# Layer norms moved from GpSimd to VectorE, with a new order of two woven streams

## The chip, the core and the metric

The kernel runs on one core of a Trainium2 chip. A core has five engines with instruction queues of their own: TensorE (PE in the profile; PEld is its weight load), VectorE (DVE), the scalar engine (ACT), GpSimd (POOL) and SyncE (SP), which here issues the DMAs. The metric is device microseconds of one execution. Matmuls write to PSUM, and the scores, products and transposes of this kernel share four PSUM slots of 128x1024 float32.

## The reference

`x` is (8, 512, 256) and the context `ctx` is (8, 1024, 192). Four residual blocks follow each other; the normed `x` of each has no learned scale:

```python
def _layernorm(x, axis=-1, eps=1e-05):
    m = jnp.mean(x, axis=axis, keepdims=True)
    v = jnp.var(x, axis=axis, keepdims=True)
    return (x - m) / jnp.sqrt(v + eps)
...
x = x + L0_xattn(_layernorm(x), ctx)   # cross attention, 16 heads of 64
x = x + L0_ffn(_layernorm(x))          # 2 of 8 experts, chosen from token 0 of each batch element
x = x + L1_xattn(_layernorm(x), ctx)   # cross attention, 16 heads of 16; the keys are the values
x = x + L1_ffn(_layernorm(x))          # weights quantized to 8 bits, activations to 16 by one global maximum
```

The last block quantizes its normed input by the largest absolute value over all batches, so it can only start when every batch has been through the three blocks before it.

## The kernel before

**Tiles.** One batch's `x` is a tile `xs[b]` of 128 partitions by 4 x 256 (four token tiles). Three of them are alive. The main part works batch by batch, a batch taking some 395 us in the middle of the run.

**Two streams.** Two generators emit the program. Stream 1 is `first_attention` for all eight batches, then the last batch's experts and half of its second attention. Stream 2 first prepares the weights of the later blocks, then runs `rest(b)` for each batch: `experts(b)`, `second_attention(b)`, `last_norm(b)`. So the first attention of a later batch runs beside the later blocks of an earlier one. Each `yield` is a step, and the text `ORDER` at the head of the file says how many steps are taken from stream 1, then from stream 2, and so on; `weave` does just that:

```python
for n, count in enumerate(ORDER.split()):
    i = n % 2
    for _ in range(int(count)):
        ...
        heads[i] = next(streams[i], None)
```

The order of TensorE's instructions is the order in which steps emit them. The other engines' instructions are put in order by the framework's scheduler. The tuples that each `yield` hands out (engine, planned microseconds, kind of hold on a buffer) are a planner's costs, with which an order was planned; they emit nothing, nor does the constant `TURN`.

**Names that matter.** In the first attention, `scores` writes `s` (L728), VectorE reduces it to `least` (L739), the scalar engine takes the exponential `e` (L741), VectorE inverts its sum to `share` (L755), GpSimd divides with it (L758), TensorE turns `e` round into `t` (L676), and the scalar engine and VectorE each copy half into `et` (L690, L688) for the product `av` (L699). `queries` and `keys` write `pq` and `pk`, `values` writes `pv`. In the second attention `sm_c` (L524) are scores for the maxima `cmx` (L531), sent through DRAM and back as the stacked rows `ck` and `m_rows`; `cav` (L1079) is the product. `tc` (L457) transposes the context that `load_ctx` loads. `acc` (L486) is a block's last matmul; `add_to_x` then adds it to `x` on VectorE (L496). At the end of the main part `tmxx` (L1274) transposes the maxima of all batches for the global scale.

**The norm.** `layernorm_T` makes three steps: the norm itself, then two chunks that transpose the normed tile on TensorE (`txn`, L418) and copy it to `xT` (L422, L427). `norm_stats` takes mean and variance on VectorE (L384, L385), and the reciprocal root on GpSimd as three rounds of Newton's method from an integer guess (L387 to L398, 14 instructions on 128x4). `normed` then subtracts and multiplies, four instructions of 128x256 on GpSimd (L409). This happens three times per batch (24 times); `last_norm` needs only the root and the row ends (`ends`), because the last block norms again on VectorE from stored statistics (L1325). The normed tile lies in the pool of `e` tiles (16 buffers).

**Other work on GpSimd** is the division, the adding of biases to `x`, two small steps on `ends`, and some memsets.

Of the kernel before, what the change touches and what calls it, by code (L numbers as in the profile page):

```python
# [14 lines left out]
ALU = mybir.AluOpType  # L15
# [4 lines left out]
EPS = 1e-5  # L20
# [4 lines left out]


ORDER = """
15 4 11 1 1 4 3 2 2 1 5 4 3 1 8 1 6 1 3 1 3 1 3 1 1 1 1 1 6 1 3 1 1 1 1 1 1 1 3 1 1
1 1 1 3 1 1 1 5 1 1 1 3 1 1 1 1 1 3 1 1 1 1 1 1 1 3 1 1 1 1 1 1 1 4 1 91 1 4 4 6 1 3
2 6 2 4 2 7 5 4 2 1 1 4 1 1 1 1 5 1 1 5 2 3 7 1 3 6 2 3 7 1 1 1 2 6 2 3 10 1 4 1 1 5  # L30
2 3 7 1 1 1 2 5 2 1 1 1 1 3 2 2 3 5 2 1 1 3 1 1 2 4 9 2 1 3 2 11 2 4 1 7 2 2 1 3 6 3
1 1 1 5 1 1 2 4 2 5 4 6 1 4 1 2 1 3 1 1 1 5 2 3 4 6 1 3 2 6 2 4 2 7 5 4 2 1 1 4 1 1
1 1 5 1 1 5 2 3 7 1 3 6 2 3 7 1 1 1 2 6 2 3 10 1 4 1 1 5 2 3 7 1 1 1 2 5 2 1 1 1 1 3
2 2 3 5 2 1 1 3 1 1 2 4 9 2 1 3 2 11 2 4 1 7 2 2 1 3 6 3 1 1 1 5 1 1 2 4 2 5 4 6 1 4
1 2 1 3 1 1 1 5 2 3 4 6 1 3 2 6 2 4 2 7 5 4 2 1 1 4 1 1 1 1 5 1 1 5 2 3 7 1 3 6 2 3
7 1 1 1 2 6 2 3 10 1 4 1 1 5 2 3 7 1 1 1 2 5 2 1 1 1 1 3 2 2 3 5 2 1 1 3 1 1 2 4 9 2
1 3 2 11 2 4 1 7 2 2 1 3 6 3 1 1 1 5 1 1 2 4 2 5 4 6 1 4 1 2 1 3 1 1 1 5 2 3 4 6 1 3
2 6 2 4 2 7 5 4 2 1 1 4 1 1 1 1 5 1 1 5 2 3 7 1 3 6 2 3 7 1 1 1 2 6 2 3 10 1 4 1 1 5
2 3 7 1 1 1 2 5 2 1 1 1 1 3 2 2 3 5 2 1 1 3 1 1 2 4 9 2 1 3 2 11 2 4 1 7 2 2 1 3 6 3
1 1 1 5 1 1 2 4 2 5 4 6 1 4 1 2 1 3 1 1 1 5 2 3 4 6 1 3 2 6 2 4 2 7 5 4 2 1 1 4 1 1  # L40
1 1 5 1 1 5 2 3 7 1 3 6 2 3 7 1 1 1 2 6 2 3 10 1 4 1 1 5 2 3 7 1 1 1 2 5 2 1 1 1 1 3
2 2 3 5 2 1 1 3 1 1 2 4 9 2 1 3 2 11 2 4 1 7 2 2 1 3 6 3 1 1 1 5 1 1 2 4 2 5 4 6 1 4
1 2 1 3 1 1 1 5 2 3 4 6 1 3 2 6 2 4 2 7 5 4 2 1 1 4 1 1 1 1 5 1 1 5 2 3 7 1 3 6 2 3
7 1 1 1 2 6 2 3 10 1 4 1 1 5 2 3 7 1 1 1 2 5 2 1 1 1 1 3 2 2 3 5 2 1 1 3 1 1 2 4 9 2
1 3 2 11 2 4 1 7 2 2 1 3 6 3 1 1 1 5 1 1 2 4 2 5 4 6 1 4 1 2 1 3 1 1 1 5 2 3 4 6 1 3
2 6 2 4 2 7 5 4 2 1 1 4 1 1 1 6 1 1 2 4 1 1 1 3 1 2 1 3 2 1 1 2 3 3 2 5 1 1 2 6 2 3
2 1 1 6 4 5 1 1 2 6 2 3 2 1 1 7 1 4 4 5 2 4 1 7 1 5 2 3 1 2 2 3 7 1 3 4 2 3 7 2 2 1
1 1 1 1 11 2 1 1 1 1 5 1 8 1 2 3 3 1 2 1 7 3 2 4 3 8 3 1 5 2 1 7 2 3 7 2 3 7 2 3 7 3
3 9 3 2 9 3 2 6 2 1 2 1 2 1 3 1 4 2
"""  # L50


# [26 lines left out]
def kernel(  # L79
# [26 lines left out]
    nc = tc.nc  # L106
# [273 lines left out]
    def norm_stats(b, mv, rs):  # L380

        st = small.tile([P, NT, 6], F32, tag="st", name="st")
        for t in range(NT):
            nc.vector.bn_stats(st[:, t, :], xs[b][:, t, :])  # L384
            nc.vector.bn_aggr(mv[:, t, :], st[:, t, :])  # L385
        ve = small.tile([P, NT], F32, tag="ve", name="ve")
        nc.gpsimd.tensor_scalar(ve, mv[:, :, 1], EPS, None, ALU.add)  # L387

        r = small.tile([P, NT], F32, tag="r0", name="r0")
        nc.gpsimd.tensor_scalar(  # L390
            r.bitcast(I32), ve.bitcast(I32), -0.5, float(0x5F3759DF), ALU.mult, ALU.add
        )
        t1 = small.tile([P, NT], F32, tag="t1", name="t1")
        for i in range(3):
            nc.gpsimd.tensor_tensor(t1, r, r, ALU.mult)
            nc.gpsimd.tensor_tensor(t1, t1, ve, ALU.mult)
            nc.gpsimd.tensor_scalar(t1, t1, -0.5, 1.5, ALU.mult, ALU.add)
            nc.gpsimd.tensor_tensor(rs if i == 2 else r, r, t1, ALU.mult)  # L398

    def norm_of(b):  # L400
        mv = small.tile([P, NT, 2], F32, tag="mv", name="mv")
        rs = small.tile([P, NT], F32, tag="rs", name="rs")
        norm_stats(b, mv, rs)
        return mv, rs

    def normed(pool, tag, b, mean, rs):
        xn = pool.tile([P, NT, D], F32, tag=tag, name=f"xn_{b}")
        for t in range(NT):
            nc.gpsimd.tensor_scalar(  # L409
                xn[:, t, :], xs[b][:, t, :], mean(t), rs(t), ALU.subtract, ALU.mult  # L410
            )
        return xn

    def transposed_chunk(b, xn, xT, c, by_place=False):

        t = bank(f"txn_{b}_{c}")
        for i in range(NT):
            nc.tensor.transpose(  # L418
                t[:, i * P : (i + 1) * P], xn[:, i, c * P : (c + 1) * P], ident
            )  # L420
        if by_place:
            nc.scalar.copy(  # L422
                xT[:, c, :].rearrange("p (w r) -> p w r", w=CD),
                t.rearrange("p (r w) -> p w r", w=CD),
            )
        else:
            nc.scalar.copy(xT[:, c, :], t)  # L427
# [3 lines left out]
    def layernorm_T(b, xT, by_place=False):  # L431

        xn = []

        def norm():
            mv, rs = norm_of(b)
            xn.append(
                normed(pp, "e", b, lambda t: mv[:, t, 0:1], lambda t: rs[:, t : t + 1])
            )

        return [(1.3, [(0, None, "dve", 2.6, None), (0, None, "pool", 8.2, "then")], norm)] + [
            (
                ("done", 0) if c == 0 else 0,
                [(0.5, "s", "act", 0.6, "full")],
                lambda c=c: transposed_chunk(b, xn[0], xT, c, by_place),
            )
            for c in range(DH)
        ]
# [124 lines left out]
    def prologue(b):  # L573

        if b in loaded:
            raws = loaded.pop(b)
        else:
            load_x(b)
            raws = load_ctx(b)
        c1 = io.tile([P, L], F32, tag="c1", name=f"c1_{b}")  # L580
        c2 = io.tile([P, L // 2], F32, tag="c2", name=f"c2_{b}")
        contexts[b] = c1, c2
        xTs[b] = work.tile([P, DH, S], F32, tag="xT", name=f"xT_{b}", bufs=1)

        def bias():
            for i in range(NT):
                nc.gpsimd.tensor_tensor(xs[b][:, i, :], xs[b][:, i, :], bo_b, ALU.add)

        return layernorm_T(b, xTs[b]) + context_T(b, raws, c1, c2), bias

    def first_attention():
# [172 lines left out]
        VALUES = [(2.75, "s", "act", 1.03, "full")]  # L764
        OUT = [(3.44, "s", "dve", 1.25, "full")]
        BIAS = [(0, None, "pool", 2.9, "aside")]
        TURN = 0.55

        share = 1 / (NP * NT)

# [8 lines left out]
        def divided(g):  # L779
            return [  # L780
                (0, None, "dve", 0.2, None, (("y", g % 4),), None),
                (0, None, "pool", 4.8, "then", (), ("w", g % 4)),
            ]

        def turned_round(g, u):
            engine, took = ("dve", 1.22) if u else ("act", 1.03)
            return [(TURN, "s", engine, took, "rows", (("w", g % 4),), ("t", u, g % 4))]

# [10 lines left out]
        for n in range(last + 2):  # L799
# [5 lines left out]
            for i in range(NT):  # L805
                g = n * NT + i
# [130 lines left out]
    def second_attention(b, pairs, last=False):  # L937
# [172 lines left out]
        def turned(g, a):  # L1110

            t = bank(f"cta_{b}_{g}")
            flat = a.rearrange("p w d -> p (w d)")
            for c in range(DH):
                nc.tensor.transpose(t[:, tok(c)], flat[:, tok(c)], ident)
            aT = small.tile([P, D], F32, tag="aT", name=f"caT_{b}_{g}", bufs=1)
            nc.vector.tensor_copy(aT, t[:, :D])
            return aT
# [26 lines left out]
        JOIN = [(0.86, "s", "dve", 1.5, "columns")]  # L1145
        TURN = [(0.3, "s", "dve", 0.4, "full")]
        OUT = [(0.86, "s", "dve", 0.4, "full")]
# [20 lines left out]
        for p in pairs:  # L1168
            for kt in range(NK):
# [11 lines left out]
                if kt == 4:  # L1181
                    yield 0, HALF[0]
                    attend(p, 0)
                    if joining:
                        yield 0, TURN
                        a = turned(p // 2 - 1, a)
# [19 lines left out]
        a = joined(p1 // 2 - 1)  # L1206
        yield ("done", 0), TURN
        a = turned(p1 // 2 - 1, a)
# [4 lines left out]
    def last_norm(b):  # L1213


        yield 1, [(0, None, "dve", 5.5, None), (0, None, "pool", 4.5, "then")]
        mv = small.tile([P, NT, 2], F32, tag="mv", name="mv")
        norm_stats(b, mv, stats[:, b, :, 1])
        nc.vector.tensor_copy(stats[:, b, :, 0], mv[:, :, 0])
        for i, op_ in enumerate((ALU.max, ALU.min)):  # L1220
            nc.vector.tensor_reduce(ends[:, b, i, :], xs[b], AX.X, op_)
        for i in range(2):
            nc.gpsimd.tensor_tensor(
                ends[:, b, i, :], ends[:, b, i, :], stats[:, b, :, 0], ALU.subtract
            )
            nc.gpsimd.tensor_tensor(
                ends[:, b, i, :], ends[:, b, i, :], stats[:, b, :, 1], ALU.mult
            )
        yield ("done", 0), []
        xd[b] = dram.tile([P, NT, D], F32, name=f"xd{b}")  # L1230
        nc.sync.dma_start(out=xd[b], in_=xs[b])
        done.add((b, "stored"))
# [239 lines left out]
```

## Time and profile before

| What | Value |
|---|---|
| Median of 3 runs | 3412.78 us (3411.16 to 3414.15) |
| Profiled execution | 3413.37 us |
| Its span | 3411.5 us |
| Mean granted TensorE clock | 0.974 |
| Normed quarters on GpSimd (L409) | 96, 1222 ns each |
| Divisions on GpSimd (L758) | 512, 1894 ns each |

The span is the time from the first to the last instruction in the trace; the execution's own time contains 1.9 us more. In a group's line the form is engine, line, operation, tiles `out<-in`, shapes and count, then total busy microseconds and mean nanoseconds of one. In the timeline's lines start and length come first, and a bracket at the end gives the idle time before the instruction and what released it.

### The profile page before, as it was taken

To read this page: it belongs to the slowest core of one execution; us is meant where nothing else is said; L and a number is where in the kernel's file an instruction comes from. 1 tells how busy PE (TensorE), PEld (TensorE's weight loads), DVE (VectorE), ACT (ScalarE), POOL (GpSimd) and SP (SyncE) were. 2 spreads that over 40 slices of the span, in tenths; PEclk is the share of its full clock that TensorE was granted. 3 is DMA by queue.
4 is the path that set the end of the run, shared out by engine and by line. 5 is a ranking of instruction groups with operands and counts; after the bars stand their busy time and mean duration, and the time that the engine had idled before them with its cause. 6 is when DMAs were issued, how large, how long until landed. Compare 5 with 4: busy or idle time off the path is not lost.

```text
span 3411.5 us, 59285 instructions
## 1 busy us (share of the span) xinstructions
PE 3183.9 (93%) x24293; PEld 1789.0 (52%) x24293; DVE 2045.0 (60%) x2583; ACT 1857.9 (54%) x2589; POOL 1282.3 (38%) x1260
## 2 busy tenths in 40 slices
PE   7899999999999999999999999999999999978887
PEld 4455555555455555555545554555555555544347
DVE  3654566546665476655665466654766456656688
ACT  4554456544556455554655455554555546544578
POOL 4355522454234622355224542345223543311002
PEclk9999999999999999999999999999999999988989
DMA  2010111011110111111110111101111111012112
GB/s 86 26 32 21 45 33 37 27 41 41 38 35 27 43 32 36 35 44 29 32 51 14 41 41 38 41 26 38 32 41 32 41 32 29 14 44 62 50 57 81
DMA packets 102649, 132.00 MB, mean 39 GB/s; under 512 B 19807, under 2 KB 82028, under 8 KB 102252
## 3 DMA queue, kind: packets, MB, share of 16 engines
q1 hardware_dynamic: 102380, 128.22, 13.7%
q8 instruction: 192, 3.15, 0.4%
q14 instruction: 77, 0.63, 0.1%
HBM read 67.34 MB, written 9.96 MB: 23 GB/s over the span
## 4 chain that ended last, share of the span: by engine, by line
PE 74%; DVE 12%; ACT 6%; POOL 3%; issue 2%; DMA 1%; SPq 1%; ACTq 0%; DVEq 0%; POOLq 0%
PE s L728 15%; PE av L699 11%; PE cav L1079 6%; PE t L676 6%; DVE cmx L531 5%; PE acc L486 5%; PE pv L512 4%; PE s_c L562 3%; PE pq L602 3%; PE pk L512 3%; ACT e L741 2%; ACT e_c L567 2%; PE sm_c L524 2%; PE s_c L565 2%; PE pv L514 2%
## 5 line engine op out<-in xcount | busy, mean ns | idle before, releaser
L758 POOL TENSOR_TENSOR e<-e,share 128x1024 f32<-128x1024 f32 x512 | 958.9, 1894 | 1559.1 <-DVE share L755 1528.0
L741 ACT ACTIVATE e<-s,least 128x1024 f32<-128x1024 f32 x512 | 569.6, 1113 | 621.3 <-DVE least L739 590.0
L739 DVE TENSOR_REDUCE least<-s 128x1 f32<-128x1024 f32 x512 | 603.2, 1219 | 229.5 <-PE s L728 226.4
L531 DVE TENSOR_REDUCE cmx<-sm_c 128x2 f32<-128x1024 f32 x512 | 602.1, 1219 | 169.8 <-PE sm_c L524 169.2
L728 PE MATMUL s<-k,q 64*128 64x512 f32 x2048 | 586.6, 624 | 23.0 <-ACT et L690 8.8
L567 ACT ACTIVATE e_c<-s_c 128x1024 f32<-128x1024 f32 x512 | 499.7, 1024 | 112.9 <-PE s_c L565 101.8
L699 PE MATMUL av<-et,v 128*64 128x256 f32 x4096 | 472.2, 384 | 0.7 <-ACT et L690 0.7
L688 DVE COPY et<-t 128x1024 f32<-128x1024 f32 x256 | 312.8, 1222 | 230.4 <-PE t L676 228.5
L699 PEld LDWEIGHTS av<-et,v 128*64 128x64 f32 x4096 | 284.4, 137 | 219.4 <-issue 67.9
L728 PEld LDWEIGHTS s<-k,q 64*128 64x128 f32 x2048 | 237.1, 191 | 221.1 <-issue 118.1
L676 PEld LDWEIGHTS t<-ident,e 64*128 64x128 f32 x8192 | 294.4, 141 | 93.9 <-issue 68.2
L690 ACT COPY et<-t 128x1024 f32<-128x1024 f32 x256 | 260.1, 1016 | 151.4 <-PE t L676 149.9
L676 PE MATMUL t<-ident,e 64*128 64x64 f32 x8192 | 313.7, 227 | 18.1 <-ACT e_c L567 12.1
L562 PE MATMUL s_c<-cq,ck 64*128 64x512 f32 x1024 | 248.5, 476 | 16.1 <-ACT e_c L567 10.7
L524 PE MATMUL sm_c<-ck,cq 64*128 64x512 f32 x1024 | 228.5, 442 | 25.9 <-DMA ck<-ckl 12.5
L1079 PE MATMUL cav<-e_c,cv 128*32 128x512 f32 x2048 | 248.2, 599 | 2.2 <-DVE cmx L531 1.9
L755 DVE RECIPROCAL share<-total 128x2 f32<-128x2 f32 x256 | 42.5, 166 | 298.2 <-ACT e L741 297.8
L565 PE MATMUL s_c<-m_rows,m_ones 64*128 64x512 f32 x1024 | 208.6, 396 | 2.7 <-DMA m_rows<-mr_c 2.6
L562 PEld LDWEIGHTS s_c<-cq,ck 64*128 64x128 f32 x1024 | 99.3, 187 | 165.2 <-issue 39.4
L524 PEld LDWEIGHTS sm_c<-ck,cq 64*128 64x128 f32 x1024 | 98.8, 189 | 107.5 <-DVE cmx L531 38.4
L512 PE MATMUL pv<-wv,c 128*128 128x256 f32 x512 | 131.2, 399 | 3.7 <-DMA wv<-in_L_xattn_w_kv_dram 2.4
L512 PE MATMUL pk<-c,wk 128*128 128x512 f32 x256 | 126.8, 618 | 4.5 <-DVE et L688 2.7
(202 smaller groups left out, 3382.9 us busy)
## 6 DMA issues: line engine op xcount, KB each, us to landing
cq<-cqs SPq DMA_DIRECT2D x256, 64.0 KB
ck<-ckh SPq DMA_DIRECT2D x112, 128.0 KB
ck<-ckl SPq DMA_DIRECT2D x112, 128.0 KB
wq<-in_L_xattn_w_q_dram SPq DMA_DIRECT2D x32, 256.0 KB
wo<-in_L_xattn_w_out_dram SPq DMA_DIRECT2D x32, 256.0 KB
w<-in_L_ffn_W_dram SPq DMA_DIRECT2D x32, 256.0 KB
x<-xd SPq DMA_DIRECT2D x16, 512.0 KB
ctx<-in_ctx_dram SPq DMA_DIRECT2D x16, 384.0 KB
```

The lines of the kernel that those rows point to most:

```text
L512: nc.tensor.matmul(out, lhs, rhs, start=first, stop=False, skip_group_check=True)
L524: nc.tensor.matmul(s[:, h, :], q[half, tok(i)], k[half, g * 512 : (g + 1) * 512], start=True, stop=True,)
L531: nc.vector.tensor_reduce(mx[:, :, i, g], s, AX.X, ALU.max)
L562: nc.tensor.matmul(s[:, h, :], k[half, tok(kt)], q[half, :], start=True, stop=False)
L567: nc.scalar.activation(e, s, AF.Exp, scale=scale)
L676: nc.tensor.transpose(t[:, w, h, kt, :], es[n, i][h][half, tok(4 * u + kt)], ident[half, half],)
L699: nc.tensor.matmul(av[h * AD : (h + 1) * AD, : S // 2], v[m][:, 4 * u + kt, (at + h) * AD : (at + h + 1) * AD], turned[n, j, u][:, h, kt]. ...
L728: nc.tensor.matmul(s[h][:, g, :], q[n][half, tok(i)], k[n][half, g * 512 : (g + 1) * 512], start=True, stop=True,)
L739: nc.vector.tensor_reduce(least[:, h : h + 1], s[h], AX.XY, ALU.min)
L741: nc.scalar.activation(e, s[h].rearrange("p g n -> p (g n)"), AF.Exp, bias=least[:, h : h + 1], scale=-1.0, accum_out=total[:, h : h + 1],)
L758: nc.gpsimd.tensor_tensor(e, e, share[:, h : h + 1].to_broadcast([P, L]), ALU.mult)
L1079: nc.tensor.matmul(av[col : col + SL, :], va[:, v : v + SL], es[p, kt][:, h, :], start=(i == 0), stop=(i == NK // 4 - 1),)
```

## The change

It has three parts. The root of `norm_stats` runs on VectorE, with one small instruction fewer in each of its three rounds and one more ahead of them (12 in all). The four instructions of `normed` run on VectorE. `ORDER` is a new list, planned with new constants for the norm, the division, `TURN` and the last norm. GpSimd keeps the divisions, the biases, `ends` and the memsets. The line numbers of the changed file are 1 higher from the table on and 3 higher after `norm_stats`.

```diff
 ORDER = """
-15 4 11 1 1 4 3 2 2 1 5 4 3 1 8 1 6 1 3 1 3 1 3 1 1 1 1 1 6 1 3 1 1 1 1 1 1 1 3 1 1
...
+16 2 10 1 5 1 1 2 5 3 3 2 8 1 1 1 4 1 1 1 5 3 11 1 4 1 3 1 3 1 1 1 3 1 1 1 1 1 1 1 4
...
 """
...
         ve = small.tile([P, NT], F32, tag="ve", name="ve")
-        nc.gpsimd.tensor_scalar(ve, mv[:, :, 1], EPS, None, ALU.add)
+        nc.vector.tensor_scalar(ve, mv[:, :, 1], EPS, None, ALU.add)
 
         r = small.tile([P, NT], F32, tag="r0", name="r0")
-        nc.gpsimd.tensor_scalar(
+        nc.vector.tensor_scalar(
             r.bitcast(I32), ve.bitcast(I32), -0.5, float(0x5F3759DF), ALU.mult, ALU.add
         )
+        nc.vector.tensor_scalar(ve, ve, -0.5, None, ALU.mult)
         t1 = small.tile([P, NT], F32, tag="t1", name="t1")
         for i in range(3):
-            nc.gpsimd.tensor_tensor(t1, r, r, ALU.mult)
-            nc.gpsimd.tensor_tensor(t1, t1, ve, ALU.mult)
-            nc.gpsimd.tensor_scalar(t1, t1, -0.5, 1.5, ALU.mult, ALU.add)
-            nc.gpsimd.tensor_tensor(rs if i == 2 else r, r, t1, ALU.mult)
+            nc.vector.tensor_tensor(t1, r, r, ALU.mult)
+            nc.vector.tensor_tensor(t1, t1, ve, ALU.mult)
+            nc.vector.scalar_tensor_tensor(
+                rs if i == 2 else r, t1, 1.5, r, ALU.add, ALU.mult
+            )
...
         for t in range(NT):
-            nc.gpsimd.tensor_scalar(
+            nc.vector.tensor_scalar(
                 xn[:, t, :], xs[b][:, t, :], mean(t), rs(t), ALU.subtract, ALU.mult
             )
...
-        return [(1.3, [(0, None, "dve", 2.6, None), (0, None, "pool", 8.2, "then")], norm)] + [
+        return [(1.3, [(0, None, "dve", 6.0, None)], norm)] + [
...
-        TURN = 0.55
+        TURN = 0.52
...
-                (0, None, "pool", 4.8, "then", (), ("w", g % 4)),
+                (0, None, "pool", 4.0, "then", (), ("w", g % 4)),
...
-        yield 1, [(0, None, "dve", 5.5, None), (0, None, "pool", 4.5, "then")]
+        yield 1, [(0, None, "dve", 7.2, None), (0, None, "pool", 1.0, "then")]
```

## The prediction

> **What bounds the kernel now.** I read the page's busy shares and chain first, then TensorE's waits, then the timeline at one wait and the granted clock around it.
>
> ```profile
> PE 3183.9 (93%) x24293; PEld 1789.0 (52%) x24293; DVE 2045.0 (60%) x2583; ACT 1857.9 (54%) x2589; POOL 1282.3 (38%) x1260
> PE 74%; DVE 12%; ACT 6%; POOL 3%; issue 2%; DMA 1%; SPq 1%; ACTq 0%; DVEq 0%; POOLq 0%
> ```
>
> TensorE is the bound. It idles 227.6 us of 3411.5, so that is all an order or a faster norm can win, and its clock a little more. Busy TensorE time is unchanged by the edit. The waits, longest total first (what TensorE waited for, us in total, times, longest):
>
> ```profile
> PE txn L418 <- POOL xn L409: 49.1, 33, 11.7
> PE sm_c L524 <- DMA ck<-ckl: 12.5, 3, 9.9
> ...
> PE tc L457 <- DMA ctx<-in_ctx_dram: 10.7, 7, 1.8
> ...
> PE tmxx L1274 <- DVE m1x L1272: 7.7, 1, 7.7
> ```
>
> The norm is the largest wait. It is in few places: 13.9 us at the start and about 5.0 in each of seven batches (35 us), always the experts' norm. The other norms have no idle TensorE. One of the seven (batch 1), TensorE and then GpSimd:
>
> ```profile
> 716.87 2.32 PE L728 MATMUL s<-k,q 64*128 64x512 f32 x8
> 719.12 3.67 PE L699 MATMUL av<-et,v 128*64 128x256 f32 x32
> 725.48 0.33 PE L418 MATMUL txn<-ident,xn 128*128 128x128 f32 x1 [2.68 <-POOL xn L409]
> 726.68 0.47 PE L418 MATMUL txn<-ident,xn 128*128 128x128 f32 x1 [0.88 <-POOL xn L409]
> 727.89 0.47 PE L418 MATMUL txn<-ident,xn 128*128 128x128 f32 x1 [0.73 <-POOL xn L409]
> 729.09 1.33 PE L418 MATMUL txn<-ident,xn 128*128 128x128 f32 x5 [0.73 <-POOL xn L409]
> ```
> ```profile
> 724.20 4.84 POOL L409 TENSOR_SCALAR xn<-x,mv,rs 128x256 f32<-128x256 f32 x4
> 729.00 3.74 POOL L758 TENSOR_TENSOR e<-e,share 128x1024 f32<-128x1024 f32 x2
> ```
>
> The last acc matmul ended at 715.9; t, s and av (7.0 us) stood before txn; the root began on GpSimd at 720.23 and the fourth normed quarter came at 729.0. The clock answers (columns: window, length, busy us and count of PE, PEld, DVE, ACT, POOL, then granted clock, DMA share, GB/s):
>
> ```profile
> 722.80:731.20 8.40, 2.84 (x12) 1.60 (x12) 0.17 (x1) 2.28 (x5) 7.96 (x11) 0.73 0.00 0
> 731.20:735.00 3.80, 3.80 (x40) 2.76 (x40) 2.56 (x6) 1.01 (x1) 1.54 (x1) 0.50 0.05 7
> ```
>
> After each 5 us stall the clock is 0.50 for 6.8 to 10.2 us; half of that, 3.4 to 5.1, is lost if TensorE alone sets the pace there; I price it at 3, since other engines are late in part of it. Gaps of 1.8 to 2.3 us (ctx) brought 3.4 us of half clock in three of seven batches, so 3 x 1.7 / 7 = 0.7 per batch.
>
> The Trainium skill, "TensorE: Matmul & The Clock Gate", § What's actually happening, gives half speed after an idle window of about 3.4 us. By that rule gaps under 3.4 us would cost no clock, and the sum below would be 1.5 us lower; the rows of the ctx gaps say otherwise, and I go by them.
>
> **The norm itself.** Removed from GpSimd: 14 small instructions at a pitch of 0.28 us (3.97 us from 720.23 to 724.20) and four of 1222 ns, 8.8 us in all. Added to VectorE: 12 small dependent ones and four normed quarters. These rows of VectorE price them:
>
> ```profile
> 3237.18 0.73 DVE L1325 TENSOR_SCALAR xn<-x,stats 128x256 f32<-128x256 f32 x2
> ...
> 3243.14 0.15 DVE L299 TENSOR_SCALAR amx<-amx 128x1 f32<-128x1 f32 x1
> 3243.33 0.16 DVE L300 RECIPROCAL sx<-amx 128x1 f32<-128x1 f32 x1
> ```
>
> The pitch of dependent small operations is 0.19, so 12 x 0.19 = 2.3; one quarter is 0.41 and each further one 0.32, so 1.4; together 3.7 us against 8.8. VectorE gains 24 x 3.7 + 8 x 2.3 = 107 us (60% to 63%); GpSimd loses 116 us of normed quarters and about 90 of roots. VectorE's 3.7 us stands in its queue ahead of the least and cmx reduces (1.22 each), for which ACT's exponentials wait and then TensorE. Its price lies between 0 (divisions start 8.8 us sooner, VectorE idles 40%) and 30 us (3.7 for one uncovered norm in each of eight batches); I take 3 us, nearest the row that shows six hidden norms with no stall.
>
> **Contention.** VectorE's single-source 128x256 operations were held when GpSimd worked (min, median, max ns):
>
> ```profile
> L306 DVE TENSOR_SCALAR wT<-wT,s_w x8: 302/348/1983, 108.5 to 114.9; 128x256 f32<-128x256 f32 x8
> ```
> ```profile
> L887 DVE TENSOR_SCALAR chosen<-idx x8: 157/794/796, 337.5 to 3036.2; 1x2 int32<-1x2 uint32 x8
> ```
>
> 1983 - 302 = 1.7 us, about one division (L758, 1894 ns mean); L887 ended at 338.30 where it began at 337.51, beside a division that ended at 338.28. The new quarters are of this sort, and divisions keep running, so each exposed norm may pay one or two: 13 norms x 1.7 to 3.4 = 22 to 44 us. I take 0 and keep the bound: at the exposed norms the last division ends 1.0 to 1.5 us after acc and the quarters start some 6 us after it.
>
> "SBUF — State Buffer", § Who interferes with whom, in the Trainium skill speaks against this change: VectorE in a two-port mode, or with two inputs from SBUF, shares a lock with GpSimd, and whoever is second stands still for a whole instruction. By that rule the root's products would be held too, and the upper end would be nearer wherever a division runs.
>
> **The order, place by place**, from the listed order of both programs. The planner's constants enter no instruction.
>
> *Start* (first txn 11.69, last quarter 15.24): stats end at 6.04, 6.04 + 3.7 = 9.7, so -5.5; weights still have to land, so 0 to -5.5, taken -5.0.
>
> *Experts' norm of batches 1 to 5.* s and av now stand behind txn, only t (1.05) before it. VectorE after acc: x add 1.25, four statistics 1.54, an et copy 1.22, aggregates 0.17, root 2.3, quarters 1.4 = 7.9, with hand-offs 8.2. TensorE's stall is about 6.2, +1.2 on today's 5.0.
>
> *Second-attention norm of batches 1 to 5.* Today 13 us of TensorE's work stands between acc and txn. In the new order av 3.6, t 1.05, pq 1.9 = 6.6, and VectorE's norm is interleaved with another batch's, 9.8 with the et copy: the last quarters are late by about 2.7, where it was 0, and about 1 us of half clock.
>
> *What else is late there.* The ctx load is issued from SP behind m_rows and lands 1.8 us late per batch; its buffer is freed 13 us ahead now: -1.85, and -0.7 of half clock. The cmx run (sm_3 to sm_7 back to back, 3.56 us for 1.15 of work) is spread between other work, -2.4; s behind et -1.0; tm behind xT -0.9. These three (-4.3) are read from the order alone, and a wait taken off one engine often leaves the next behind it: half, -2.15. So a batch stands at 1.2 + 2.7 + 1.0 - 0.7 - 1.85 - 2.15 = +0.2; five: +1.0.
>
> *Batch 0*: the first norm stalls 2 (was 4.75), the second 5.3 (was 0), with clock +2.5. *Batch 6*: t, s, av, t, s, pv stand before both norms, 5.0 and 3 of clock go: -8. *Tail*: the waits from 3019 to 3050 sum to 15.4, 9.9 of them the ck load queued on SP behind the last batch's router reads and expert weights; the router now comes earlier, its own norm is exposed by 5 and the ck wait falls by half: -5. *End*: the 7.7 us wait before tmxx stands behind the last norm's root, 3.97 on GpSimd and 2.3 on VectorE: -1.6.
>
> Sum: -5.0 + 3 + 1.0 + 2.5 - 8 - 5 - 1.6 = -13.1. From the profiled execution, 3413.4 us (1.9 outside its span), that is 3400.3; it stands 0.6 above the median of 3412.8, so 3399.7, rounded to 3400.
>
> **The rivals.**
>
> *Two exposed norms and nothing back* (slower). The places between acc and txn shrank from 7.0 and 13 to 1.05 and 6.6 us. If the -1.85, -0.7 and -2.15 per batch do not come, each of five batches loses 4.9, +24.5; with batch 0 +2.5, VectorE +3, and -5, -8, -5, -1.6: +10.4, 3423. With VectorE's term doubled and no gain in the tail, 3431. It decides once the other waits fall by less than 10.4 / 5 = 2.1 us per batch, where I took 4.7. For it: three of the four credits are read from the order, not from a row; against it, the ctx row is a load whose buffer comes free earlier in the listed order. Chance 0.21.
>
> *The lock* (slower): +22 to +44 on -13.1, so 3422 to 3444. For it, the two lines above; against it, 0.41 us quarters at L1325 beside GpSimd's small work only. It decides from 13.1 / 13 = 1.0 us per exposed norm. Chance 0.12.
>
> *All covered*: the order finds 8 us of work for each norm after all; stalls -35, start -5.5, clock 7 x 3 = -21: 3351. The 1.05 and 6.6 us counted above speak against it. Chance 0.07.
>
> *Nothing net*: the planner's 6.0 for VectorE against my 8.2 is off by 2.2, twice in five batches 22 us, about what is won: 3412. Chance 0.13. That the change does not move the norm can be excluded: the listing shows all 16 instructions on VectorE.
>
> **How the numbers follow.** My forecast has 0.47. Its own range takes full credit for the order waits (5 x 2.15 = 10.75: 3389) and none of the tail, with VectorE's term doubled (3408). The 8 in 10 range leaves out the fully covered case and the upper half of the lock: 3370 to 3432. A measurement can tell 0.2%, 6.8 us, from no change. Faster (under 3406): 0.44 of the forecast and 0.07, 0.51; same: 0.03 of the forecast, 0.10 of nothing net, 0.01 of the slower rival, 0.14; slower: 0.20 + 0.12 + 0.03 = 0.35.
>
> **What would show it.** Right: xn on VectorE of about 0.4 us, no row of POOL before txn; batch 1's txn waits 6 us, its second norm's 2 to 3; tc behind ctx gone; the start's last quarter at about 9.7; batch 6 without 0.50 clock. Wrong: quarters or small root operations over 1 us beside L758 (the lock); second norms hidden (too pessimistic), or a new wait on least or cmx that outgrows 3 us (VectorE becomes late).

## The result, and the profile after

The changed kernel takes 3420.55 us (median of 12 runs, 3416.91 to 3425.03) against 3413.47 (12 runs) before: ratio 1.0022, 95% interval 1.0013 to 1.0031. It is slower by 7 us. The range of the prediction held it; the side did not. Two of its slower cases come near: "two exposed norms and nothing back" with 3423, and the lower end of "the lock" with 3422.

The page of the changed kernel, and what TensorE waited for:

```profile
PE 3192.5 (93%) x24293; PEld 1778.1 (52%) x24293; DVE 2145.3 (63%) x3063; ACT 1856.3 (54%) x2587; POOL 1082.2 (32%) x716
```
```profile
PE txn L421 <- DVE xn L412: 60.9, 29, 9.1
PE av L702 <- ACT e L744: 17.9, 13, 2.4
...
PE tc L460 <- ACT e L744: 8.7, 7, 1.6
...
PE tmxx L1277 <- DVE m1x L1275: 7.4, 1, 7.4
```

VectorE is busy 100 us more, GpSimd 200 less, as the prediction had it. TensorE's idle time is the same (3421.1 - 3192.5 = 228.6, before 227.6), though the norm now takes 3.7 us instead of 8.8: the wait for xn rose from 49.1 to 60.9, and a wait of av for the exponentials is new. TensorE's busy time rose by 8.6 with the same matmuls. The clock accounts for that: summed from the trace's clock records, the time that TensorE was busy at half clock rose from 118.2 to 140.8 us, and half of this rise is 11 us.

The experts' norm of batch 1 and, below the dots, the second-attention norm beside it (start, length, then the group; idle time ahead of it in brackets):

```profile
715.22 1.21 PE L679 MATMUL t<-ident,e 64*128 64x64 f32 x32
722.24 2.21 PE L421 MATMUL txn<-ident,xn 128*128 128x128 f32 x8 [5.81 <-DVE xn L412]
...
763.21 1.98 PE L605 MATMUL pq<-xT,wq 128*128 128x512 f32 x4
766.52 0.56 PE L421 MATMUL txn<-ident,xn 128*128 128x128 f32 x2 [1.32 <-DVE xn L412]
767.48 0.33 PE L421 MATMUL txn<-ident,xn 128*128 128x128 f32 x1 [0.40 <-DVE xn L412]
768.22 1.33 PE L421 MATMUL txn<-ident,xn 128*128 128x128 f32 x5 [0.41 <-DVE xn L412]
```

5.81 us (forecast 6.2) and 1.32 + 0.40 + 0.41 = 2.13 us (forecast 2.7). The second wait had been 0. What VectorE did ahead of it, thinned:

```profile
762.14 0.15 DVE L388 TENSOR_SCALAR ve<-mv 128x4 f32<-128x4 f32 x1
...
763.61 0.17 DVE L388 TENSOR_SCALAR ve<-mv 128x4 f32<-128x4 f32 x1
...
764.64 1.22 DVE L691 COPY et<-t 128x1024 f32<-128x1024 f32 x1
765.77 0.15 DVE L399 SCALAR_TENSOR_TENSOR rs<-t,r 128x4 f32<-128x4 f32 x1
...
765.96 2.20 DVE L412 TENSOR_SCALAR xn<-x,mv,rs 128x256 f32<-128x256 f32 x4
...
769.88 0.17 DVE L399 SCALAR_TENSOR_TENSOR rs<-t,r 128x4 f32<-128x4 f32 x1
```

Two roots begin, at 762.14 and 763.61, and two `rs` end. The second belongs to the first norm of a later batch, whose quarters come only at 1017 us; the scheduler issues it here, where its statistics are ready. And the four quarters take 2.20 us where the experts' take 1.38 (721.68 to 723.06). GpSimd's bias adds (x + cbo_b) stand beside them:

```profile
766.52 2.92 POOL L961 TENSOR_TENSOR x<-x,cbo_b 128x256 f32<-128x256 f32 x4 [7.58 <-DVE xn L412]
```

Granted clock (the number before the last two) around the two waits:

```profile
716.50:722.30 5.80, 0.06 (x1) 0.09 (x1) 5.35 (x24) 0.49 (x1) 0.00 (x0) 0.84 0.15 42
722.30:726.00 3.70, 3.15 (x14) 2.06 (x16) 1.30 (x7) 1.17 (x2) 0.00 (x0) 0.50 0.00 0
...
768.20:772.00 3.80, 3.79 (x9) 2.10 (x9) 1.71 (x5) 1.17 (x2) 1.24 (x2) 0.55 0.00 0
```

By stage, from one batch's route matmul (the first one behind its experts' norm) to another's: the length, the idle time ahead of TensorE's matmuls and the time that TensorE was busy with the clock at 0.50, summed from the trace's gaps and clock records (these gaps sum to a few us less than span minus busy time).

| Stage | before: length, idle, busy at half clock | after |
|---|---|---|
| start to route 1 | 730.3, 55.7, 20.8 | 724.4, 54.6, 23.3 |
| route 1 to route 5 (four periods) | 1581.1, 71.6, 35.6 | 1596.8, 82.2, 46.6 |
| route 5 to the end | 1100.0, 94.7, 61.8 | 1100.0, 86.4, 70.9 |

The new order has one s and one av (1.99 + 3.67 us) behind route that were ahead of it, so 5.7 us of work moved from the first stage to the last. Without that the stages stand at -0.3, +15.7 and -5.7: the sum is the +9.7 of the two profiled spans. The steady batches lose it: 3.9 us each, about 2.6 of them idle and 11.0 / 4 / 2 = 1.4 of half clock.

### The profile page after: what moved, and what is told of

Read it like the earlier page. It is cut to its first block, busy times and chain, and to the rows that moved or that the text cites. A ratio compares the mean times of both kernels' runs of the same rounds, so it can differ in the third digit from the quotient of the medians.

```text
span 3421.1 us, 59304 instructions
## 1 busy us (share of the span) xinstructions
PE 3192.5 (93%) x24293; PEld 1778.1 (52%) x24293; DVE 2145.3 (63%) x3063; ACT 1856.3 (54%) x2587; POOL 1082.2 (32%) x716
## 5 line engine op out<-in xcount | busy, mean ns | idle before, releaser
L731 PE MATMUL s<-k,q 64*128 64x512 f32 x2048 | 581.6, 625 | 13.1 <-ACT k L636 7.3
L702 PE MATMUL av<-et,v 128*64 128x256 f32 x4096 | 476.3, 386 | 30.9 <-ACT e L744 17.9
L679 PE MATMUL t<-ident,e 64*128 64x64 f32 x8192 | 306.7, 224 | 15.3 <-ACT e L744 6.3
L605 PE MATMUL pq<-xT,wq 128*128 128x512 f32 x256 | 131.2, 636 | 1.4 <-ACT e L744 0.4
```

Source lines behind the costliest of these rows:

```text
L679: nc.tensor.transpose(t[:, w, h, kt, :], es[n, i][h][half, tok(4 * u + kt)], ident[half, half],)
L702: nc.tensor.matmul(av[h * AD : (h + 1) * AD, : S // 2], v[m][:, 4 * u + kt, (at + h) * AD : (at + h + 1) * AD], turned[n, j, u][:, h, kt]. ...
L731: nc.tensor.matmul(s[h][:, g, :], q[n][half, tok(i)], k[n][half, g * 512 : (g + 1) * 512], start=True, stop=True,)
```

## The experiments

Theory A: the order is what loses. Theory B: VectorE's longer queue and its lock with GpSimd lose. Ratios are to the kernel before in the same session; 1% is 34 us.

**1. Both halves apart.** The norm of the change with the order of before; the order of the change with the norm of before; and, in the old order, root or quarters alone on VectorE.

```diff
 both_old_order:      ORDER = the list of before; norm_stats and normed on nc.vector
 neither_new_order:   ORDER = the new list;       norm_stats and normed on nc.gpsimd
 root_old_order:      ORDER = the list of before; norm_stats on nc.vector, normed on nc.gpsimd
 quarters_old_order:  ORDER = the list of before; norm_stats on nc.gpsimd, normed on nc.vector
```

> Root and normed quarters on VectorE as in the changed kernel, order as before. Theory A (the new order is what loses): the start gains 4.75 us as measured after the change, each of the seven experts' norms keeps 7.0 us of TensorE work ahead, but VectorE's queue puts the two least reduces (2.4 us) inside the root, so the chain is 8.2 + 2.4 = 10.6 and the stall 3.6 instead of 5.0: 7 x 1.4 = 10 less; the end 1.6 less. About 3413 - 16 = 3397. Theory B (VectorE's longer queue and its lock with GpSimd lose, the order does not): the 20 us that quarters lost to divisions and 100 us more of VectorE show as new waits behind least and cmx with this order too, and the time is 3420 or more.

> The order of the change, root and quarters on GpSimd as before. Theory A: the narrow places between acc and txn (1.05 and 6.6 us of TensorE work) now meet GpSimd's 8.8 us instead of VectorE's 3.7, so experts' norms stall about 10.9 instead of 5.8 and second norms about 5.5 instead of 2.1, in five batches 42 us, with 5 at the start and 5 in the tail about 3470; the other waits of the new order (exponential before av, 2.8 us a batch) stay. Theory B: taking 100 us off VectorE and the lock away brings back what was lost, 3400 to 3415.

> Only the root on VectorE, quarters on GpSimd, order as before. Root with two least reduces inside it is 2.3 + 2.4 = 4.7 us against 3.97 on GpSimd, so each experts' norm is 0.7 us later (5 us in seven), the start 1.6 and the end 1.6 earlier: 3411 to 3416 by theory A. Theory B: small operations with two SBUF inputs are held by divisions too, some 1 us or more per norm: over 3420.

> Only the normed quarters on VectorE, root on GpSimd, order as before. The least reduces run while GpSimd takes the root, so the chain is 4.3 + 4.0 + 1.5 = 9.8 us after acc against 13.1 before: each of seven stalls falls from 5.0 to about 1.7 (23 us), the start by 3.4, some half clock goes with it (up to 3 us each): 3413 - 26 = 3387, down to 3370 with the clock, by theory A. Theory B: quarters beside divisions take 0.8 to 2 us each in the hidden norms and the reduces behind them are late; the gain is halved or gone, 3400 to 3413.

Measured: 3414.1 us, ratio 1.0012 (1.0002 to 1.0022); 3474.4, 1.0185 (1.0171 to 1.0199); 3440.9, 1.0087 (1.0074 to 1.0101); 3427.9, 1.0053 (1.0039 to 1.0067). The second run lies on theory A's 3470: the new order is made for a short norm and costs 63 us with a long one. But with the old order the short norm brings nothing (4 us slower), where I expected 16 less, and either half alone on VectorE is slower still (with the root alone the wait of s that is shown below stands at the second norm too, and with the quarters alone txn waits for exponentials, 12.3 us in all, and route for xT, 16.6). The old order has the same matmuls in the same sequence in both kernels, so time can be compared matmul by matmul. In both_old_order each experts' txn wait fell from 5.0 to 2.2 us, below the expected 3.6, and the whole idle time from 227.6 to 212.0. The loss is at the second norm, where before had no clock loss:

```profile
769.33 1.26 PE L678 MATMUL t<-ident,e 64*128 64x64 f32 x32
772.39 4.43 PE L730 MATMUL s<-k,q 64*128 64x512 f32 x8 [1.80 <-ACT e L743]
776.75 3.78 PE L514 MATMUL pv<-wv,c 128*128 128x256 f32 x8
```
```profile
770.60:772.40 1.80, 0.01 (x1) 0.01 (x1) 1.78 (x18) 1.79 (x4) 0.00 (x0) 1.00 0.00 0
772.40:776.00 3.60, 3.60 (x8) 1.25 (x8) 3.53 (x7) 1.93 (x3) 2.91 (x4) 0.72 0.00 0
776.00:780.50 4.50, 4.50 (x11) 2.56 (x10) 3.98 (x8) 1.46 (x3) 2.59 (x2) 0.50 0.00 0
```

pv takes 3.78 us, nearly twice its time at full clock (2.00 in before), and s 4.43 against 2.24, a part of which is a wait for its second exponential. A wait of 1.8 us, 1.4 more than before, and the half clock behind it: matmul by matmul this place costs 4.7 to 6.2 us in each of batches 0 to 5.

**2. Which queue makes s wait?** In both_old_order the scalar engine copies `av` into `o` before the exponentials that s waits for:

```profile
769.45 0.38 ACT L710 COPY o<-av 128x256 f32<-128x256 f32 x1 [11.27 <-PE av L701]
769.84 1.28 ACT L743 ACT_TABLE_LOAD   x1
771.13 1.11 ACT L743 ACTIVATE e<-s,least 128x1024 f32<-128x1024 f32 x1
```

Before, the copy came behind them. Nothing in the change touches that engine; VectorE's new work made the scheduler place it so. Theory P: that is the cause. Theory Q: VectorE's queue is late itself. The pin, and three placements:

```diff
+                with tc.issue_after(exps[n + 1, 0]):
+                    nc.scalar.copy(part, av[:, : S // 2])
...
 old_order_pinned:             the pin in batches 1 to 6, otherwise both_old_order
 next_norm_aside_old_order:    first norms of batches 1 to 7 on nc.gpsimd
 experts_norm_only_old_order:  on nc.vector: batch 0's first norm, all experts' norms, the very last norm
 next_norm_aside_new_order:    the changed kernel, first norms of batches 1 to 7 on nc.gpsimd
```

> As both_old_order, but in batches 1 to 6 the scalar engine's copy of av into o is issued behind the exponentials of the next scores, as it stood before the norm moved; its whole queue then has the order of before. Theory P (the scheduler put that copy ahead of the exponentials, which then wait for av; 1.8 us of TensorE wait and about 4 us of half clock follow in each of six batches): both go, 3414 - 25 to 30 = 3384 to 3389. Theory Q (VectorE's queue is late itself: the norm and the next batch's root stand ahead of the next least, and the copy is only a sign of it): the wait moves a few us behind, 3405 to 3415.

> Old order; the first norm of batches 1 to 7, which has some 240 us of slack, stays on GpSimd, the experts', second and last norms are on VectorE. The scalar engine still copies o ahead of the exponentials. Theory P: the wait of 1.8 us and its half clock stay, 3408 to 3415. Theory Q: VectorE's queue loses the next batch's root in the middle of the second norm and the 4 us that its quarters lost beside divisions, so the next least is up to 4 us earlier: 3385 to 3395.

> Old order; only the norms that TensorE waited for are on VectorE: the first of batch 0, the experts' of all batches, the last of the last batch. All others stay on GpSimd. The queues of the scalar engine and of VectorE keep the order of before, apart from the norm. Both theories: the start gains 4.7, each experts' norm 2.8 to 3.4 in seven batches, the second norm loses nothing, the end 1.6: 3413 - 28 = 3385, less if shorter stalls also spare half clock. A third theory, that a shorter stall comes back as a wait elsewhere in the batch, gives 3400 to 3410.

> The changed kernel with its new order, but the first norm of batches 1 to 7 stays on GpSimd. If VectorE's load and its lock with GpSimd lost the time in the new order, the second norm's stall falls from 2.1 us to about 0.5 (its root is no longer interleaved with another) and the reduces beside the hidden norm come 5 us earlier: 3405 to 3412. If the order itself loses (5.8 us at the experts' norm and 2.4 at av behind the exponential per batch), it stays between 3414 and 3421.

Measured: 3422.9 us, 1.0036 (1.0023 to 1.0048); 3407.3, 0.9980 (0.9971 to 0.9989); 3380.3, 0.9909 (0.9894 to 0.9924); 3402.8, 0.9977 (0.9968 to 0.9986). Theory P falls: with the pin the wait of s is gone and a larger one stands behind it.

```profile
770.32 2.24 PE L735 MATMUL s<-k,q 64*128 64x512 f32 x8
...
777.67 1.12 PE L420 MATMUL txn<-ident,xn 128*128 128x128 f32 x4 [2.12 <-DVE et L690]
780.10 1.12 PE L420 MATMUL txn<-ident,xn 128*128 128x128 f32 x4 [1.31 <-ACT e L748]
```

VectorE's et copy and the next least stand behind the norm and the other root, so txn, which needs a PSUM slot that they free, is late instead. The trace names et and e as what txn waits for, not xn: it is short of a PSUM slot, which they free. That is theory Q. But taking the next norm away alone (3407) gives 7 us (11 by the ratios) where theory Q had 19 to 29: the second norm itself is dear, too. The third run keeps every norm that nobody waited for on GpSimd and is 31 us faster than before:

```profile
715.22 1.64 PE L428 MATMUL txn<-ident,xn 128*128 128x128 f32 x8 [2.20 <-DVE xn L419]
```
```profile
PE 3177.3 (94%) x24293; PEld 1782.1 (53%) x24293; DVE 2076.9 (61%) x2739; ACT 1858.6 (55%) x2589; POOL 1211.0 (36%) x1084
```

The experts' stall is 2.2 as in both_old_order, idle time is 3379.0 - 3177.3 = 201.7 (26 less than before), and TensorE's busy time is 6.6 us below before instead of 16 above. The fourth run gains 15 us on the changed kernel by its ratio, and the trace had to say by what.

**3. The two suspects in the new order.** What of the next batch's first norm is dear there, its root (woven into the second norm) or its quarters (held by divisions)? Is the narrow place before the experts' txn a loss of its own? And is a covered second norm dear without any other norm on VectorE?

```diff
 next_quarters_aside_new_order:  the changed kernel; of these first norms only normed on nc.gpsimd
 next_root_aside_new_order:      the changed kernel; of these first norms only the root on nc.gpsimd
 s_av_ahead_new_order:           the changed kernel; ORDER, in batches 1 to 5:
-3 3 1 1 6
+5 3 1 1 4
 second_norm_only_old_order:     ORDER = the list of before; second norms on nc.vector, all others on nc.gpsimd
```

> The changed kernel; of the first norm of batches 1 to 7 only the four normed quarters stay on GpSimd, its root is on VectorE. next_norm_aside_new_order gained some 17 us with both aside. If the quarters held by divisions (5.6 instead of 1.4 us, with the reduces behind them) were the price, this run keeps most of the gain: 3403 to 3408. If the root was, because it is woven into the second norm and delays its rs by about 1.5 us a batch, it keeps little: 3414 to 3420.

> The counterpart: of the first norm of batches 1 to 7 only the root stays on GpSimd, its quarters are on VectorE. If the quarters and their lock were the price: 3414 to 3420. If the root woven into the second norm was: 3403 to 3408. Both about halfway (3409 to 3413) if they add.

> The changed kernel; in batches 1 to 5 the next scores s and one av, which the new order has behind txn, are put ahead of it, as in the old order. If the narrow place is what the stall of 5.8 us comes from, 7.0 us of TensorE work now stand before txn and the stall is about 2.2, as in both_old_order: 5 x 3.6 = 18 less, 3402, and with 3 us less of half clock in each, down to 3394. If the work that is moved is missed behind txn (route waits for xT, the exponentials are late for the next t), half of that: about 3411.

> Old order; only the second-attention norms are on VectorE, every other norm is on GpSimd as before. They had no idle TensorE before. Between next_norm_aside_old_order (3407) and experts_norm_only_old_order (3380) the second and the last norms made 27 us. If a covered norm on VectorE is that dear by itself, this run is slower than before by 15 to 27 us: 3426 to 3438, with s waiting 1.8 us for the exponential at the second norm and half clock after it. If the loss needs the experts' norm on VectorE too (order of the queues), it is within 5 us of before.

Measured: 3416.7 us, 1.0018 (1.0008 to 1.0028); 3403.3, 0.9979 (0.9970 to 0.9989); 3393.8, 0.9948 (0.9932 to 0.9965); 3439.1, 1.0083 (1.0066 to 1.0100). Taking the root alone aside gives the time of root and quarters aside (3402.8); taking the quarters alone aside gives next to nothing. Yet those quarters are slow, as the group in the changed kernel and one covered norm on VectorE and GpSimd show:

```profile
L412 DVE TENSOR_SCALAR xn<-x,mv,rs 128x256 f32<-128x256 f32 x96 | 58.6, 666 | 0.4
```
```profile
1017.37 0.40 DVE L412 TENSOR_SCALAR xn<-x,mv,rs 128x256 f32<-128x256 f32 x1
...
1020.05 2.93 DVE L412 TENSOR_SCALAR xn<-x,mv,rs 128x256 f32<-128x256 f32 x3
```
```profile
1017.53 3.84 POOL L761 TENSOR_TENSOR e<-e,share 128x1024 f32<-128x1024 f32 x2 [5.53 <-DVE share L758]
1021.33 2.92 POOL L590 TENSOR_TENSOR x<-x,bo_b 128x256 f32<-128x256 f32 x4
```

2.93 us for three quarters here, 1.38 for four alone: VectorE is held. But nobody waits for these, and the second run says that it costs nothing. So I took the root, woven into the urgent second norm, for the price. Its removal shows this there:

```profile
763.39 1.64 PE L429 MATMUL txn<-ident,xn 128*128 128x128 f32 x8 [1.21 <-DVE xn L420]
```

(next_norm_aside_new_order), 0.92 us less than 2.13. Of these 0.82 are the quarters, which take 1.38 again, and only 0.1 the root's place: with the root on GpSimd its bias adds come behind the root, at 764.78, when the quarters are done. Experiment 5 settles which it is. The waits alone are small: between the changed kernel and next_root_aside_new_order the gaps ahead of TensorE's matmuls sum to 223.1 and 221.5, but its busy time at half clock to 140.8 and 96.1, 45 us less; its busy time falls by 19.6, and the spans are 3421.1 and 3399.9.

The narrow place is a loss of its own. With s and av ahead of it, txn waits 2.07 instead of 5.81 in batch 1, and the wait for xn over the whole run is

```profile
PE txn L422 <- DVE xn L413: 42.5, 29, 9.0
```

against 60.9: 18 less, as forecast; the time falls by 25 us by the ratios, the rest being mostly clock (busy at half clock 107.8 us, against 140.8). second_norm_only_old_order repeats the s wait of 1.80 us and loses 28 us with one norm per batch on VectorE, one that had no idle TensorE before.

**4. Both repairs at once,** because together they are more than the change lost: the edit of s_av_ahead_new_order with the first norms of next_norm_aside_new_order.

> New order with s and av ahead of the experts' txn in batches 1 to 5, and the first norm of batches 1 to 7 wholly on GpSimd. If the two causes are separate, their gains add: 3420.5 - 26.7 - 17.7 = 3376. If they share one wait or one stretch of half clock, the second repair brings less than half of its own: 3385 to 3394.

Measured: 3382.0 us, ratio 0.9916 (0.9900 to 0.9933). By the ratios to before, the changed kernel stands at +7.5 us, s_av_ahead at -17.7, next_norm_aside at -7.8, both at -28.7: 25.2 + 15.3 = 40.5 expected, 36.2 found. They are two losses, nearly additive. This kernel and experts_norm_only_old_order (0.9909) are as fast as each other within their intervals: the new order brought nothing that the old one, with VectorE's norm where it was waited for, did not.

**5. Root or bias adds?** GpSimd's four adds are put behind the last quarter, by one small operation of GpSimd that reads it; the queues of VectorE and the scalar engine stay as they were.

```diff
+            late = small.tile([P, 1], F32, tag="late", name=f"late_{b}", bufs=1)
+            gate = nc.gpsimd.tensor_scalar(late, xn3[b][0][:, NT - 1, 0:1], 1.0, None, ALU.mult)
+            with tc.issue_after(gate.ins):
                 for i in range(NT):
...
 bias_behind_quarters_new_order: in the changed kernel; bias_behind_quarters_old_order: in both_old_order
```

> The changed kernel; GpSimd's four bias adds of the second attention (x + cbo_b) are issued behind one 128x1 operation that reads the last normed quarter, so they start when all four quarters are done. Nothing else moves: the queues of VectorE and the scalar engine are the same. In the changed kernel the adds start after the first quarter, and the last two quarters take 0.81 instead of 0.41 us beside them. If that is why the next norm's root was dear on VectorE (on GpSimd it keeps the adds back until the quarters are through), the quarters take 1.4 instead of 2.2 us, the wait of the second txn falls from 2.13 to 1.3, and most of next_root_aside's 15 us comes: 3404 to 3410. If the root's place in VectorE's queue is the price, it stays at 3417 to 3421.

> The same edit in both_old_order. There the quarters of the second norm also take 2.2 us, but txn has more work ahead of it; s waits 1.8 us for an exponential that stands behind the copy of av, ahead of the quarters in time. If the lock on the quarters matters there, the et copy and the next least behind them are 0.8 us earlier and some of the six half-clock stretches go: 3400 to 3408. If the wait of s alone makes the half clock: within 4 us of both_old_order, 3410 to 3416.

Measured: 3404.8 us, ratio 0.9982 (0.9972 to 0.9991); 3411.5, 1.0003 (0.9994 to 1.0012). In the new order the adds alone were 14 us by the ratios: nearly all of what the root's move had brought. VectorE, GpSimd and TensorE at batch 1's second norm now:

```profile
767.11 1.38 DVE L412 TENSOR_SCALAR xn<-x,mv,rs 128x256 f32<-128x256 f32 x4
```
```profile
768.58 0.23 POOL L962 TENSOR_SCALAR late<-xn 128x1 f32<-128x1 f32 x1 [8.49 <-DVE t L398]
```
```profile
767.67 1.64 PE L421 MATMUL txn<-ident,xn 128*128 128x128 f32 x8 [1.32 <-DVE xn L412]
```

1.38 us, and one wait of 1.32 instead of three that sum to 2.13, as expected. The root is still woven in, and costs little. The clock makes most of the 14 us: idle time falls only from 228.6 to 226.0, while TensorE's busy time falls from 3192.5 to 3179.3 and the part of it at half clock from 140.8 to 112.9. In the old order, where more work covers the second txn, the edit brings 3 us, which the two intervals do not tell apart from nothing.

## Why the prediction was wrong

*The norm, the start.* Right. 3.7 us was 3.62 where nothing stood beside it (719.44 to 723.06: root 2.24, quarters 1.38); the last quarter of the start came at 10.08 (forecast 9.7). Start and batch 0 together were forecast at -2.5 and measured -0.3 after the work that changed stage.

*Contention.* This step failed, and what it left out is more than the whole loss. It was priced at 0 because in the kernel before the divisions were through when the exposed quarters would start. In the changed kernel that held for the experts' norms of batches 1 to 5 and 7, but not for those of batches 0 and 6. VectorE and GpSimd in batch 0:

```profile
326.00 4.54 DVE L412 TENSOR_SCALAR xn<-x,mv,rs 128x256 f32<-128x256 f32 x4
```
```profile
326.14 3.92 POOL L761 TENSOR_TENSOR e<-e,share 128x1024 f32<-128x1024 f32 x2 [7.68 <-DVE share L758]
```

The four quarters took 4.54 us instead of 1.38, in batch 6 too; what that cost was not tried. And divisions are not all that GpSimd does: the bias adds into the same `x` wait for the first quarter and then run beside the others. Each second norm's quarters lost 0.82 us to them, 5 us in the six exposed places, and together with the half clock behind it 14 us by the ratios. Without the adds beside the quarters the changed kernel is 6 us faster than before by its ratio, where 13 were forecast. The rival "the lock" had the mechanism right. Its size was off: 14 us where it had 22 to 44, from a shorter hold in six places instead of one or two divisions in 13. What was missing was the place, which the diff does not show and the list of GpSimd's work does. The Trainium skill, "SBUF — State Buffer", § Who interferes with whom, gives the lock for VectorE instructions in a two-port mode, which `tensor_scalar` can enter, and for those with two inputs from SBUF. The trace agrees on VectorE's side: beside the adds a quarter takes 0.82 us instead of 0.41, and a product of the other root 0.69 (768.08) instead of 0.16. It adds that the covered quarters, held far longer, cost nothing that the intervals show.

*Experts' and second norm, batches 1 to 5.* Near: 5.8 and 2.1 us against 6.2 and 2.7. The second is in part luck, because 0.8 of the 2.1 is the contention that the forecast had at 0; with the adds behind the quarters it is 1.3, half of what was forecast. Over before the two make +2.9 us per batch, forecast +3.9. The narrow place that the forecast counted was there: undoing it brought 25 us.

*What else is late there.* This step failed too. It credited 1.85 us for ctx and half of 4.3 us for waits that the new order spreads, 4.0 per batch. The waits for ctx, of s for et (8.8 us in all) and of tm for xT (6.0) did go; that of sm_c for cmx did not (6.8 before, 9.4 after). And others took their place: tc waits for an exponential (8.7 us, ctx had 10.7), and av for exponentials (17.9 us, 2.4 the longest). Idle time rose by 10.6 us in four periods where the norm's waits rose by 4 x 2.9 = 11.7, so 0.3 us per batch were left of the 4.0, with the contention's waits in the 11.7. Over five batches some 18 us did not come, an estimate from one trace of each kernel. Even the halving that stood there as caution was too kind. The rival "nothing back" had this right (it decided below 2.1 us per batch); that its 3423 lies so near the result is luck, as it has no contention in it, and with the adds behind the quarters the kernel takes 3405.

*Clock.* The forecast had +0.3 us per batch; it was +1.4, and -0.8 with the adds behind the quarters (29.1 us busy at half clock in the four periods, against 46.6 and, before, 35.6).

*VectorE's queue.* Taken at 3 us. In the new order, leaving the next norm's root and quarters off VectorE brought 1 to 2 us more than moving the bias adds, within the intervals of both; the term was small there. In the old order it was not: one covered second norm per batch on VectorE cost 28 us, near the upper bound of 30. The row it was priced from, hidden norms with no stall, showed norms on GpSimd, where they were in nobody's way.

*Batch 6, tail, end.* -14.6 forecast, -5.7 measured, and -11.7 with the bias adds behind the quarters (stages from route 5: 406.7 + 308.4 + 209.3 + 169.6 = 1094.0 against 1100.0, less 5.7). The ck load's wait did go (sm_c behind ck: 12.5 us before, 0.6 after); tmxx waits 7.4 instead of 7.7, so of the 1.6 at the end 0.3 came.

In sum: -13.1 forecast, +9.7 between the profiled spans. Of these 22.8 us the bias adds are 15.8 (spans 3421.1 and 3405.3). With the adds behind the quarters the three stages are 725.3, 1586.1 and 1094.0 us long, so they stand at +0.6, +5.0 and -11.7, where -2.5, +0.8 and -14.4 (batch 5 in it) were forecast, and 3 for VectorE's queue in no stage. In the four steady periods idle time is then 8.4 us above before and the norm's two waits 8.5, so nothing of the credits is left; norm waits and half clock below the forecast (1.8 and 1.1 us per batch) hide most of that.

## What to carry to other kernels

Before moving an operation to VectorE, list everything that GpSimd may do beside it, what the moved operation itself releases first of all, and not only the engine's largest group. Move it only where somebody waits for it: with all norms moved the old order lost 4 us, with only the waited-for norms it gained 31, because a covered operation on a busier engine can stand ahead of urgent work. And credit a vanished wait only when the next late event is named.

## What the runs showed of the hardware

A short wait of TensorE can cost more clock than time: after 1.80 us ahead of s in both_old_order the clock stood at 0.50 from 776.0 to 780.5 and was partly down from 772.4. The length of the wait does not decide it alone: in the changed kernel av waited 2.38 us at 807.6 and the clock stayed full.

```profile
807.70:811.00 3.30, 3.30 (x32) 2.10 (x32) 0.97 (x2) 0.97 (x2) 1.99 (x2) 1.00 0.00 0
```

The Trainium skill, "TensorE: Matmul & The Clock Gate", § What's actually happening, speaks of a whole idle window of about 3.4 us; here waits of half that were enough at some places. The same wait also had different outcomes: the 1.80 us ahead of s was followed within 2 us by 6.8 us at 0.50 in batches 0, 1, 3 and 5 of both_old_order and not in batches 2 and 4, and the 1.32 us of bias_behind_quarters_new_order by 3.4 us at 0.50 in batch 1 and by none in batches 2 to 5. In each of the 17 traces all stretches at 0.50 begin on one grid of 3.41 us and, the last one aside, last a whole multiple of it. So where a wait falls on this grid counts beside its length, and a mere shift in time can move half clock. How much of a stretch must be idle to trip it was not tried.
